# The first layer's scan as masked triangular products over blocks of 31 positions

## The chip, the core and the metric

The kernel runs on one core of one Trainium2 chip. TensorE (PE) multiplies matrices and transposes, with its weight loads (PEld) listed by themselves; VectorE (DVE) and ScalarE (ACT) work element by element and can read PSUM, into which TensorE writes; GpSimd (POOL) works on SBUF alone; SyncE (SP) issues the transfers (DMA). The metric is device time in microseconds of one launch, lower being better.

## What is computed

Two layers, each with a residual: group norm, a projection into a branch u and a gate, a state-space scan of u in four directions, a layer norm times the silu of the gate, and a projection back. The change is in the first layer's scan. Cut to that:

```python
# per batch (4), direction k (4), channel d (384), state n (16), along L = 4096 positions
xs = stack([x_hw, x_wh, flip(x_hw), flip(x_wh)])      # rows, columns, both reversed
x_dbl = einsum('bkdl,kcd->bkcl', xs, x_proj_weight)   # 12 rows for the step, 16 B, 16 C
delta = softplus(einsum(dts, dt_projs_weight) + bias)
As = -exp(A_logs)                                     # A_logs = log(1..16) for every channel
def step(h, inp):
    dA = exp(dt[..., None] * A_k[None])
    dBu = dt[..., None] * bt[:, :, None, :] * ut[..., None]
    h = dA * h + dBu
    y = einsum('bkdn,bkn->bkd', h, ct)
    return (h, y)
```

The outputs of the four directions are turned back to the order of the image and added, with u times the sum of the four D vectors. All data is f32.

## The kernel before

`FirstLayer.run` goes through the four batches one after another. `between` (L451) does what lies around the scans: `finish_steps` of the batch before, interleaved with `project_steps` (L529) of the batch to come. A projection normalizes the batch (`norm`), then handles 8 chunks of 512 positions: u by `in_proj` (L519), transposes of u (L545) into uT and into y times the D sum, and the rows of step, B and C for both orders (L556). The gate isn't projected there: `scans` does it on the side (`gate_in`, L791 writes it out).

`scans` takes 32 items (4 directions x 8 chunks of 512 positions) with 16 states each, so 512 steps a batch and 2048 in all. A step holds 3 x 128 channels by 512 positions:

- ACT multiplies the transposed dt*u by B (`b_product`, L716, four instructions) and takes exp(dt*A) (`decay`, L728, three);
- TensorE transposes the product, 12 blocks of 128 x 128, into PSUM (`turn_x`, L733);
- DVE runs the recurrence itself, one `tensor_tensor_scan` for each 128 channels (L741), and keeps the last column as a carry (L751);
- POOL multiplies h by C (L755), whose rows come from DRAM broadcast over the partitions;
- TensorE transposes h back, 12 blocks, adding over the 16 states in PSUM (`add_y`, L763).

The preparation of an item (`Item.steps`) is spread over the steps of the items before it: dt by small products (L632), softplus in parts on ACT and POOL (L638 to L658), dt*u (L681). The order on TensorE, ACT, DVE and POOL is written out by hand (`manual_schedule`); SP's is not. The second layer (`SecondLayer`, a subclass that uses `norm`, `in_proj`, `finish` and `finish_steps`) runs after all batches are done, and a flag `alive` decides at the end whether a general version of it is run too.

Of the kernel before, what the change touches and what calls it, by code (L numbers as in the profile page):

```python
# [19 lines left out]
LC = 512  # L20
# [8 lines left out]
ALL_ZERO = -105.0  # L29

# [372 lines left out]
class FirstLayer:  # L403

    def __init__(self, tc, ctx, consts, w, gate, dram):
        nc = tc.nc
        self.tc, self.w = tc, w
        self.ident, self.group, self.one = consts  # L410
        self.gate = gate
        self.uT_dram, self.ys, self.xp_dram = dram
        wp = ctx.enter_context(tc.tile_pool(name="wf", bufs=1))

        def load(name, shape):
            t = wp.tile(shape, F32, name=f"{name}_f")
            nc.sync.dma_start(t, w[name])
            return t

        self.w_xp = load("w_xq2", [128, ND, 2, 2 * NX])  # L420
        self.w_dt = load("w_dtb", [DR + 1, KD, DI])
        self.gamma = load("gamma", [128, ND])
        self.beta = load("beta", [128, ND])
        self.A = load("A_log", [128, KD, ND, NS])
        nc.scalar.activation(self.A, self.A, AF.Exp)
        nc.vector.tensor_scalar_mul(self.A, self.A, -1.0)
        self.xbias = load("x_bias2", [2 * NX, 1])
        self.ln_eps = wp.tile([128, 1], F32, name="ln_eps_f")
        nc.vector.memset(self.ln_eps, 1e-6)
        self.gn_eps = wp.tile([128, 1], F32, name="gn_eps_f")  # L430
        nc.vector.memset(self.gn_eps, GN_EPS)
        self.dsum = wp.tile([128, DI], F32, name="dsum_f")
        with tc.tile_pool(name="d4", bufs=1) as pd:
            d4 = pd.tile([128, KD, DI], F32, name="d4")
            nc.sync.dma_start(d4, w["D_rows"].partition_broadcast(128))
            nc.vector.tensor_add(self.dsum, d4[:, 0, :], d4[:, 1, :])
            nc.vector.tensor_add(self.dsum, self.dsum, d4[:, 2, :])
            nc.vector.tensor_add(self.dsum, self.dsum, d4[:, 3, :])

    def run(self, srcs, dsts):  # L440
        with self.tc.tile_pool(name="xT", bufs=1) as px:
            self.xT = px.tile([CB, NC2, L], F32, name="xT")
            self.w_in = px.tile([CB, NC2, 2 * DI], F32, name="w_in")
            self.bias = px.tile([128, 2 * ND], F32, name="bias")
            for b in range(len(srcs) + 1):
                self.between([(srcs[b - 1], dsts[b - 1], self.ys[b - 1], self.gate)] if b else [], srcs[b : b + 1], b)
                if b < len(srcs):
                    self.y_dram = self.ys[b]
                    self.scans()

    def between(self, done, todo, b):  # L451

        tc = self.tc
        with ExitStack() as ctx:
            pool = lambda name, bufs, **k: ctx.enter_context(tc.tile_pool(name=name, bufs=bufs, **k))
            psum = lambda name, bufs: pool(name, bufs, space=bass.MemoryType.PSUM)
            steps = []
            if done:
                sbuf = pool("fy", 8), pool("fz", 3), pool("fl", 2), pool("fs", 1), pool("fw", 2)
                banks = (2, 2) if todo else (4, 4)  # L460
                steps.append(self.finish_steps(done, sbuf, (psum("fm", banks[0]), psum("fo", banks[1])), pool("fc", 1)))
# [4 lines left out]
            while steps:  # L466
                for g in list(steps):
                    if next(g, None) is None:
                        steps.remove(g)
# [1148 lines left out]
```

## Time and profile before

| | |
|---|---|
| three runs | 11,063.09 us median, 11,059.26 to 11,072.16 |
| span of the profiled execution | 11,060.3 us |
| instructions | 169,780 |
| mean granted TensorE clock | 0.918 |
| HBM read, written | 955.83 MB, 300.42 MB |

How a page is read: busy time of an engine is the union of its instructions; the groups that follow give line, engine, operation, output and inputs, shape, count, then busy time, mean ns of one, and the idle time of the engine before them with what ended it. A mean can hold overlap with the neighbour, above all on TensorE, whose ends are modelled; there the spacing of neighbours in time is the cost. In the timeline, a line is one stretch: start, length, engine, line, operation, count. In a table of stretches each line gives the busy time and instructions of each engine, the granted clock and the DMA share.

The rows that the change touches, besides those shown below: L632 (the products for dt, 13 rows of weights, 512 columns) is 881.8 us busy in 1536 records; L641 and L652, an exponential and a logarithm of 128 x 1536 on ACT, take 1478 and 1485 ns; L645, a scalar operation of that size on POOL, 1480 ns; L681 and L778 on DVE, 128 x 512 with one input in PSUM, 674 ns; L549, 384 columns, 554 ns; L547, a copy of 384 columns out of PSUM on ACT, 483 ns.

### The profile page before, as it was taken

Reading aid. Unit: us, or ns where it says so; the run is one execution under the profiler, and the core shown is the slowest. Engines: PE = TensorE matmul, PEld = TensorE weight load, DVE = VectorE, ACT = ScalarE, POOL = GpSimd, SP = SyncE. Lnnn points to the kernel's source line nnn. Section 1 sums busy time; section 2 is a strip of 40 time slices with the busy share of each in tenths; the row PEclk is TensorE's granted clock in tenths of the full one; section 3 lists DMA queues with packets and bytes.
Section 4 is the critical chain, followed back from the end, with each engine's and each line's share of the span. In section 5 each row is a group of like instructions: output and inputs, shape, how many; then the busy total and the mean of one; then the engine's idle time right before and its main releaser. Section 6 shows DMA issues by size and latency. Waiting matters only on the chain. (4 is left out here: it accounts for less than half of the span.)

```text
span 11060.3 us, 169780 instructions
## 1 busy us (share of the span) xinstructions
PE 9381.9 (85%) x60297; PEld 7300.4 (66%) x60297; DVE 9708.2 (88%) x11512; ACT 9816.8 (89%) x17003; POOL 8590.8 (78%) x2776
## 2 busy tenths in 40 slices
PE   7888888888888888888888888888888888778677
PEld 4776776666777776656776766657767766644366
DVE  4999999976999999968999999959999999879675
ACT  5999999977999999968999999959999999867477
POOL 3999999955999999938999999929999999700370
PEclk8999999988999999998999999989999999988688
DMA  3333344444333444443433444443333444433458
GB/s 123 108 108 98 98 98 100 98 142 127 108 105 97 101 98 98 100 163 106 109 101 98 100 99 98 99 166 109 106 98 98 99 101 98 123 116 124 159 130 277
DMA packets 833662, 1267.39 MB, mean 115 GB/s; under 512 B 102026, under 2 KB 517655, under 8 KB 832292
## 3 DMA queue, kind: packets, MB, share of 16 engines
q1 hardware_dynamic: 827940, 1250.15, 41.6%
q0 software_dynamic: 4864, 6.29, 0.4%
q8 instruction: 479, 7.85, 0.3%
q14 instruction: 379, 3.10, 0.1%
HBM read 955.83 MB, written 300.42 MB: 114 GB/s over the span
## 5 line engine op out<-in xcount | busy, mean ns | idle before, releaser
L755 POOL TENSOR_TENSOR h<-h,bct 128x1536 f32<-128x1536 f32 x2048 | 7066.0, 3473 | 550.0 <-DVE carry L751 508.2
L741 DVE TENSOR_TENSOR_SCAN h<-a,carry,x 128x512 f32<-128x512 f32 x5376 | 6615.6, 1267 | 274.7 <-PE x L733 224.1
L733 PE MATMUL x<-ident,xT 128*128 128x128 f32 x24576 | 4118.0, 293 | 982.4 <-DVE h L741 881.1
L716 ACT ACTIVATE xT<-dtuT,bT 128x384 f32<-128x384 f32 x8192 | 4358.2, 609 | 34.7 <-PE x L733 29.7
L733 PEld LDWEIGHTS x<-ident,xT 128*128 128x128 f32 x24576 | 2888.9, 148 | 2170.3 <-DVE h L741 1013.3
L728 ACT ACTIVATE a<-dt,A_log_f 128x512 f32<-128x512 f32 x6144 | 3976.7, 716 | 0.0
L763 PE MATMUL yp<-ident,h 128*128 128x128 f32 x24576 | 3839.9, 285 | 9.2 <-POOL h L755 9.2
L763 PEld LDWEIGHTS yp<-ident,h 128*128 128x128 f32 x24576 | 3079.1, 149 | 11.1 <-POOL h L755 11.1
L632 PE MATMUL dp<-xd,w_dtb_f 13*128 13x512 f32 x1536 | 881.8, 657 | 201.5 <-DVE dt L661 198.4
L741 DVE TENSOR_TENSOR_SCAN h<-a,x 128x512 f32<-128x512 f32 x768 | 897.4, 1207 | 103.2 <-ACT a L728 70.6
L645 POOL TENSOR_SCALAR wl<-e 128x1536 f32<-128x1536 f32 x128 | 189.4, 1480 | 793.8 <-ACT e L641 600.3
L519 PE MATMUL pp<-xT,w_in 96*128 96x512 f32 x1152 | 542.1, 619 | 21.8 <-ACT pad L1109 21.0
L632 PEld LDWEIGHTS dp<-xd,w_dtb_f 13*128 13x128 f32 x1536 | 232.4, 187 | 441.7 <-DVE dt L661 327.7
L638 ACT ACTIVATE e<-dp 128x512 f32<-128x512 f32 x384 | 225.0, 586 | 288.9 <-DVE dt L661 191.1
L1123 DVE SCALAR_TENSOR_TENSOR acc<-pad,conv_w_s,acc 128x2048 f32<-128x2048 f32 x192 | 440.6, 2342 | 46.2 <-ACT acc L1121 44.9
L658 POOL TENSOR_TENSOR e<-e,wl 128x1536 f32<-128x1536 f32 x128 | 445.4, 3480 | 0.3
L1104 POOL MEMSET pad<- 128x66 f32 x12 | 1.9, 160 | 570.9 <-DVE acc L1123 446.0
L655 POOL TENSOR_TENSOR e<-e,dt 128x1536 f32<-128x1536 f32 x128 | 443.2, 3463 | 0.3
L519 PEld LDWEIGHTS pp<-xT,w_in 96*128 96x128 f32 x1152 | 221.4, 199 | 264.9 <-issue 232.0
L751 DVE TENSOR_REDUCE carry<-h 128x3 f32<-128x3 f32 x2048 | 322.8, 158 | 70.4
L661 DVE SCALAR_TENSOR_TENSOR dt<-dp,e 128x512 f32<-128x512 f32 x384 | 255.6, 666 | 64.8 <-POOL e L658 58.2
L931 PE MATMUL op<-w_out,v 128*128 128x192 f32 x1536 | 292.1, 340 | 10.1 <-DVE v L921 7.1
(168 smaller groups left out, 6366.1 us busy)
## 6 DMA issues: line engine op xcount, KB each, us to landing
bct<-xp SPq DMA_DIRECT2D x1024, 512.0 KB, 5.0
uT<-uT SPq DMA_DIRECT2D x64, 768.0 KB, 4.7
yold<-y SPq DMA_DIRECT2D x64, 768.0 KB, 7.9
y<-yt SPq DMA_DIRECT2D x64, 768.0 KB, 4.5
uT<-uT SPq DMA_DIRECT2D x128, 384.0 KB, 5.3
yold<-y SPq DMA_DIRECT2D x128, 384.0 KB, 6.9
y<-yt SPq DMA_DIRECT2D x128, 384.0 KB, 4.6
zg<-gate SPq DMA_DIRECT2D x64, 768.0 KB, 5.6
```

The source lines that it names most:

```text
L519: self.tc.nc.tensor.matmul(pp, self.w_in[:, i, e * 128 : (e + 1) * 128], self.xT[:, i, t * LC : (t + 1) * LC], start=(i == 0), stop=(i == ...
L632: nc.tensor.matmul(self.dp[d], w, self.xd[0 : DR + 1, :], start=True, stop=True)
L655: nc.gpsimd.tensor_tensor(self.e, self.e, self.dt, ALU.subtract)
L658: nc.gpsimd.tensor_tensor(self.e, self.e, self.wl, ALU.add)
L716: nc.scalar.mul(xTs[g][:, j, :], it.dtuT[:, j * DI : (j + 1) * DI], it.bT[:, j, n : n + 1])
L728: nc.scalar.activation(as_[g][:, d, :], it.dt[:, d, :], AF.Exp, scale=scale)
L733: nc.tensor.transpose(xs[g, d][:, j * 128 : (j + 1) * 128], xTs[g][:, j, d * 128 : (d + 1) * 128], ident)
L741: nc.vector.tensor_tensor_scan(along(hs[g][:, d, :], it.k), along(as_[g][:, d, :], it.k), along(xs.pop((g, d)), it.k), 0.0 if it.first els ...
L751: nc.vector.tensor_reduce(kept, last(hs[g], it.k), mybir.AxisListType.X, ALU.max)
L755: nc.gpsimd.tensor_tensor(hs[g], hs[g], bc(cs[g - n % 2][:, n % 2, :], 1, ND), ALU.mult)
L763: nc.tensor.matmul(it.yp[b][:, i * 128 : (i + 1) * 128], hs[g][:, d, j * 128 : (j + 1) * 128], ident, start=n == 0 and i == 0, stop=n == N ...
L1123: nc.vector.scalar_tensor_tensor(acc, part(tap), weight(tap), acc, ALU.mult, ALU.add)
```

## The change

`FirstLayer` no longer goes batch by batch. `run` projects all four batches, then scans all batches and directions together, then finishes all batches. What `FirstLayer` and `SecondLayer` share moves into a class `Stage`.

In the new `scans` the 128 partitions hold 4 directions x 31 positions (`NP` = 124) and four more rows, one for each direction, for the state carried from block to block; the 1536 columns are 4 batches x 384 channels. A round is one block of 31 positions in each direction (133 rounds), and each has 16 steps, one for each state, 2128 steps in all. With cum, the running sum of dt in the block (less a shift of 2.5), state n of the recurrence is exp(-n cum) times the running sum of B dt u exp(n cum). The factor exp(n cum) isn't computed for each state: `grown` multiplies what state n-1 had by g = exp(cum) once more. The running sum over positions, with B, is a product with a 128 x 128 triangular mask times B (`b_mask`, `mix`), one product for each batch; `weigh` multiplies the result by C and by exp(-n cum); `add_y` adds the states in PSUM by products with the identity. The carry rows go out to DRAM after each step and come back 16 steps later.

This needs A to be n times the same value, and the sum of dt over a block to stay small. `FirstLayer` checks both (and that the variance is finite) and keeps the outcome in `good`; if it fails, the general version of both layers is run at the end. There is thus a second branch behind the kernel.

```diff
+RW = 31
+NR = -(-L // RW)
+NP = KD * RW
+W = NB * DI
+SHIFT = 2.5
+REACH = 118.0
...
+    def run(self, srcs, dsts, gates):
+        self.project(srcs, gates)
+        self.scans()
+        self.reach()
+        self.finish([(src, dst, (self.y_row[:, b, :], self.y_col[:, b, :]), gates[b]) for b, (src, dst) in enumerate(zip(srcs, dsts))])
+
+    def load_y(self, y, t, py, pl, pos):
...
+        nc.sync.dma_start(yt, pos(y[0], t))
...
+        for s in range(2):
+            nc.sync.dma_start(yc[s * HW : (s + 1) * HW], v[s])
+        nc.gpsimd.tensor_tensor(yt, yt, yc, ALU.add)
...
+    def reach(self):
...
+            nc.sync.dma_start(t, self.tot.rearrange("(p f) -> p f", p=128))
...
+            nc.vector.tensor_reduce(top, t, mybir.AxisListType.X, ALU.max)
+            nc.vector.tensor_scalar(top, top, REACH / NS - SHIFT, None, ALU.is_le)
...
+    def project(self, srcs, gates):
...
+                    for e in range(ND):
+                        nc.scalar.activation(u[:, e, :], in_proj(e, t), AF.Identity, bias=bias[:, e : e + 1])
...
+                        for e in range(ND):
+                            nc.tensor.transpose(q[:, e * 128 : (e + 1) * 128], u[:, e, part], self.ident)
+                        nc.scalar.copy(ut[:, j, :], q)
+                        nc.vector.tensor_mul(du[:, j, :], q, self.dsum)
+                        for e in range(ND):
+                            nc.tensor.matmul(
+                                bp[:, j, :], u[:, e, part], self.w_bc[:, e, :], start=(e == 0), stop=(e == ND - 1)
+                            )
...
+                    for e in range(ND):
+                        nc.tensor.matmul(xp, self.w_xd[:, e, :], u[:, e, :], start=(e == 0), stop=(e == ND - 1))
...
+                    for e in range(ND):
+                        nc.scalar.activation(zg[:, e, :], in_proj(ND + e, t), AF.Identity, bias=bias[:, ND + e : ND + e + 1])
...
+            p_x, p_e, p_t, p_b = pool("bx", 7), pool("be", 4), pool("bt", 4), pool("bb", 3)
+            ps_y = pool("psy", 1, space=bass.MemoryType.PSUM)
+            ps_q = pool("psq", 3, space=bass.MemoryType.PSUM)
...
+                def v(self, i):
+                    self.vp = ps_m.tile([128, LC], F32, name="vp", tag="m")
+                    nc.tensor.matmul(self.vp[:NP, :DI], xd[:, i, :], w_dt, start=True, stop=True)
...
+                    nc.scalar.activation(self.e[:, cols(i)], self.vp[:NP, :DI], AF.Abs)
+                    nc.scalar.activation(self.dt[:, cols(i)], self.vp[:NP, :DI], AF.Relu)
...
+                    terms = ((ident, self.e), (minus, self.d), (ident, self.l), (ident, self.dt))
+                    for j, (m, t) in enumerate(terms):
+                        nc.tensor.matmul(self.dp[:NP, :DI], m[:NP, :NP], t[:, cols(i)], start=j == 0, stop=j == 3)
...
+                    nc.tensor.matmul(self.cp[:, :DI], tri[:NP], self.dt[:, cols(i)], start=True, stop=True)
...
+                    r = [(-31, "sp", self.load_xd), (-22, "sp", self.load_u), (-11, "sp", self.load_bc)]
+                    r += [(-15, "act", self.exp), (-14, "act", self.log), (-14, "pool", self.plus)]
+                    for i in range(NB):
+                        r += [(i - 20, "pe", s(self.v, i)), (i - 19, "act", s(self.parts, i))]
+                        r += [(i - 13, "pe", s(self.delta, i)), (i - 12, "dve", s(self.times_u, i))]
+                        r += [(i - 12, "act", s(self.keep_dt, i)), (i - 8, "pe", s(self.sums, i))]
+                        r += [(i - 7, "act", s(self.keep_sums, i))]
+                    r += [(-3, "act", self.grow), (-2, "first", self.grow_psum), (-2, "sp", self.keep_total)]
+                    r += [(6, "sp", self.load_y), (NS + LAG + 1, "sp", self.store_y)]
+                    for j in range(ND):
+                        r += [(NS + LAG, f"dve{j}", s(self.end_y, j))]
...
+            def decay(s):
+                it, n = of(s)
+                es[s] = p_e.tile([128, W], F32, name="e")
+                nc.scalar.activation(es[s], it.cum, AF.Exp, scale=-(n + 1.0))
+
+            def b_mask(s, i):
...
+                if i < 2:
+                    nc.scalar.mul(bs[s][:, i, :], mask, b)
+                else:
+                    nc.gpsimd.tensor_scalar(bs[s][:, i, :], mask, b, None, ALU.mult)
+
+            def grown(s, engine):
+                it, n = of(s)
+                part = slice(0, FREE) if engine is nc.vector else slice(FREE, W)
+                x = it.dtu if n == 0 else xs[s - 1][:NP]
+                g = it.g0[:NP, :FREE] if engine is nc.vector else it.g
+                engine.tensor_tensor(xs[s][:NP, part], x[:, part], g, ALU.mult)
+
+            def mix(s, i):
+                qs[s, i] = ps_q.tile([128, LC], F32, name="q")
+                nc.tensor.matmul(qs[s, i][:, :DI], bs[s][:, i, :], xs[s][:, cols(i)], start=True, stop=True)
+
+            def weigh(s, i):
...
+                nc.vector.scalar_tensor_tensor(
+                    ts[s][:, cols(i)],
+                    qs.pop((s, i))[:, :DI],
+                    it.bc[:, i, NS + n : NS + n + 1],
+                    es[s][:, cols(i)],
+                    ALU.mult,
+                    ALU.mult,
+                )
+
+            def add_y(s, j):
...
+                nc.tensor.matmul(
+                    it.yp[j],
+                    ident,
+                    ts[s][:, j * LC : (j + 1) * LC],
+                    start=n == 0,
+                    stop=n == NS - 1,
+                    skip_group_check=True,
+                )
...
+                for s in range(-LEAD, N + LAG + 3):
+                    on = lambda q: 0 <= q < N
+                    if on(s - 1):
+                        carry_out(s - 1)
+                    if on(s + 4):
+                        carry_in(s + 4)
+                    planned(s, "sp")
+                    planned(s, "first")
+                    if on(s + 2):
+                        decay(s + 2)
+                        b_mask(s + 2, 0)
+                        b_mask(s + 2, 1)
+                    planned(s, "act")
+                    if on(s + 2):
+                        grown(s + 2, nc.gpsimd)
+                        b_mask(s + 2, 2)
+                        b_mask(s + 2, 3)
+                    planned(s, "pool")
+                    for i in range(NB):
+                        if on(s):
+                            weigh(s, i)
+                        planned(s, f"dve{i}")
+                        if i == 1 and on(s + 2):
+                            grown(s + 2, nc.vector)
+                    planned(s, "dve")
+                    for i in range(NB):
+                        if on(s + 1):
+                            mix(s + 1, i)
+                        if i > 0 and on(s - LAG):
+                            add_y(s - LAG, i - 1)
+                    planned(s, "pe")
```

SP's order is now written by hand as well. The gate is projected in `project`, with the rest, into one DRAM array for each batch; the finish loads two sums, by rows and by columns, where it loaded one.

## The prediction

> **What bounds the kernel now.** I began with the busy table at the head of the page, then took one of the four scan stages by itself, then the costliest groups, and last the order in time on TensorE. The head of the page and the scan stages of the first two batches (columns: from and to, length, then busy time and instructions of PE, weight loads, DVE, ACT and POOL, granted clock, DMA share, GB/s):
>
> ```profile
> PE 9381.9 (85%) x60297; PEld 7300.4 (66%) x60297; DVE 9708.2 (88%) x11512; ACT 9816.8 (89%) x17003; POOL 8590.8 (78%) x2776
> ...
> 205.00:2370.00 2165.00, 1885.57 (x13095) 1527.34 (x13095) 2063.01 (x2330) 2100.43 (x3713) 2033.18 (x628) 0.95 0.40 100
> 2610.00:4790.00 2180.00, 1900.02 (x13175) 1537.95 (x13176) 2078.26 (x2347) 2113.95 (x3737) 2051.17 (x632) 0.94 0.39 100
> ```
>
> In a scan stage ACT is 97% busy, DVE 95%, POOL 94%, PE 87%. A batch has 512 steps, and 2180/512 is 4.26 us a step. No single engine sets it; all four are loaded to nearly the same level, so a change must be added up for every engine. These groups make up the step:
>
> ```profile
> L755 POOL TENSOR_TENSOR h<-h,bct 128x1536 f32<-128x1536 f32 x2048 | 7066.0, 3473 | 550.0 <-DVE carry L751 508.2
> L741 DVE TENSOR_TENSOR_SCAN h<-a,carry,x 128x512 f32<-128x512 f32 x5376 | 6615.6, 1267 | 274.7 <-PE x L733 224.1
> L733 PE MATMUL x<-ident,xT 128*128 128x128 f32 x24576 | 4118.0, 293 | 982.4 <-DVE h L741 881.1
> L716 ACT ACTIVATE xT<-dtuT,bT 128x384 f32<-128x384 f32 x8192 | 4358.2, 609 | 34.7 <-PE x L733 29.7
> L728 ACT ACTIVATE a<-dt,A_log_f 128x512 f32<-128x512 f32 x6144 | 3976.7, 716 | 0.0
> L763 PE MATMUL yp<-ident,h 128*128 128x128 f32 x24576 | 3839.9, 285 | 9.2 <-POOL h L755 9.2
> ```
>
> All of TensorE's work in a step is transposes: 12 at L733 and 12 at L763 (24576/2048), one record each. What one costs is read from its neighbours in time, since the mean of 293 ns overlaps with the next. In the scan, weight loads of four come 0.44 us apart (columns: start, length, engine, line):
>
> ```profile
> 1201.52 0.47 PEld L733 LDWEIGHTS x<-ident,xT 128*128 128x128 f32 x4
> ...
> 1201.96 0.47 PEld L763 LDWEIGHTS yp<-ident,h 128*128 128x128 f32 x4
> ...
> 1202.40 0.47 PEld L733 LDWEIGHTS x<-ident,xT 128*128 128x128 f32 x4
> ```
>
> So a 128-column transpose takes 110 ns, and the step 24 x 0.11 = 2.64 us of TensorE. Ordinary f32 products are another matter, and the change is made of them. The projections show them. Two things are to be seen: how many records one product leaves, and how far apart they are.
>
> ```profile
> L556 PE MATMUL xp<-u,w_xq_f 128*128 128x512 f32 x384 | 178.0, 593 | 0.0
> ```
>
> L556 runs 3 products for 2 orders, 8 chunks and 4 batches: 192 products, yet 384 records. An ordinary f32 product is two records, each with its own weight load; a transpose is one. L519's gate products (192, 384 records) and L931's (768, 1536 records) say the same. The spacing of a dense row of 512-column records, and of 192-column ones:
>
> ```profile
> 10002.13 0.19 PEld L519 LDWEIGHTS pp<-xT,w_in 96*128 96x128 f32 x1 [0.24 <-issue]
> 10002.56 0.19 PEld L519 LDWEIGHTS pp<-xT,w_in 96*128 96x128 f32 x1 [0.24 <-issue]
> 10002.99 0.19 PEld L519 LDWEIGHTS pp<-xT,w_in 96*128 96x128 f32 x1 [0.24 <-issue]
> ...
> 10999.70 10.48 PE L931 MATMUL op<-w_out,v 128*128 128x192 f32 x55
> ```
>
> 512 columns: 430 ns a record, the 190 ns load hidden behind the product before. 192 columns: 10.48/55 = 190 ns a record, the length of the load. So a 512-column product costs 0.86 us. The granted clock of such dense stretches:
>
> ```profile
> 80.00:90.00 10.00, 9.99 (x33) 5.09 (x32) 3.87 (x6) 3.10 (x6) 0.00 (x0) 1.00 0.50 185
> 90.00:100.00 10.00, 9.99 (x33) 4.97 (x32) 3.80 (x6) 3.10 (x6) 0.00 (x0) 1.00 0.50 184
> ```
>
> **The change, part by part.** The four scan stages (181.5 us, the first scan, to about 2380; the last ends at 9636; some 2195 us each), the three stages between them (some 222 us each) and the first projection go. In their place stand one projection of all batches, 133 rounds x 16 = 2128 steps, and one finish.
>
> *TensorE in a step.* mix is four products of 384 columns, add_y three of 512. A 384-column record is in no row of before: in proportion to 512 it is 322.5 ns; on the line through 190 (192 columns) and 430 it is 334. I take 322.5, since 190 is the load's length and not the product's; the other end adds (8 + 3) x 11.5 ns x 2128 = 270 us. mix: 8 x 322.5 = 2.58 us. add_y: 6 x 430 = 2.58 us. Each round adds v 4, delta 16, sums 4, 24 products of 384 columns or 48 records: 15.48 us, 0.97 a step. Together 6.13 us a step against 2.64 before; 133 rounds of 98.0 us are 13,039 us.
>
> *The other engines in a step* lie behind that. POOL: the 1152-column product, 2605 ns by proportion to L755 or 2718 on the line through 1461 ns for 512 columns (L1302); two masks of 128 columns, each between 160 ns (a memset of 66) and 1480 ns (L645, 1536), taken near the small end as 300; plus, 1480/16. Sum 3.3 us, and with every upper end 5.8. ACT: decay 1478 (L641), two masks between 303 (L1131, 128 columns) and 609 (L716), a sixteenth of the round's 8 x 483 + 1478 + 1485 + 4 x 483 + 4 x 580 + 1108 + 500 (483 from L547, 580 from L540's 686 by 384 of 512 columns and its start, 1485 from L652): 2.9 to 3.5 us. DVE: five of 384 columns at 554 (L549) and a sixteenth of 4 x 554 + 3 x 674: 3.0 us. SP issues some 70 transfers a round (32 carries, 4 xd, about 9 each for u and bc, about 6 and 8 for y, 1 total); before, they follow each other on its queue at 0.32 to 0.45 us, so 32 of 98 us. If TensorE did not cover them, POOL would be next at 3.3 us.
>
> *Waits added.* mix waits for the masks and for grown, one step older on ACT and POOL, and for one of three q buffers, which weigh frees. DVE needs 3 us in 6. end_y for a round sits between the weighs and holds the three y banks, which the next round's first add_y needs; 0.67 us each, and TensorE has two mixes (1.3 us) in front of it. The carry is read back 12 steps after it was written, 70 us; queued behind a late one on SP would be u, bc and y, for which whole steps are free. I price these at 1% of the stage, 130 us: between none (9.99 of 10 us above) and the 5% that PE missed in a dense stretch of the second layer (47.71 of 50 us at 9950).
>
> *Projection.* To the first product, 40 us as now. A chunk has 15 products of 512 columns (in_proj 6 for u and 6 for the gate, now out in the open, xp 3): 30 x 0.43 = 12.9 us; 12 transposes, 1.4; 12 products of 128 columns for B and C, 24 records at the load's 190 ns, 4.6. 18.9 x 32 = 604. Three more norms at some 15: 45. Sum 689. ACT (6 us) and DVE (5 us a chunk) are hidden.
>
> *Around the scan.* Filling took about 60 us before (135 to 195); I keep it, and 10 for draining. reach loads 3.3 MB, which at the finish's 316 GB/s is 10 us, and a reduction: 15.
>
> *Finish.* The second layer's finish moves 2.36 MB a chunk and takes 239 us for 32 chunks (10821 to the end), at a DMA share near 0.95: transfers set it. The column sums add 0.79 MB a chunk: 239 x 3.15/2.36 = 319 us. POOL's added sum, 3.5 us a chunk, is hidden.
>
> *The rest.* Second layer from about 9722 to the end: 1338, and 5 for the second flag. The sum of any 31 neighbouring step sizes, worked out from the reference's inputs, is at most 4.9, below the 7.4 that the flag allows, so the general path isn't run.
>
> Sum: 689 + 60 + 13,039 + 10 + 130 + 15 + 319 + 1343 = 15,605 us of the profiled execution, whose own span of before, 11,060.3, is 3 us under the median of the runs; so 15,600.
>
> Two statements of the Trainium skill bear on this. "TensorE: Matmul & The Clock Gate", section "Back-to-back issue gap", gives a sustained 131 ns for 512 columns; by it a step would need, as an estimate, some 2.2 us of TensorE, POOL would set it at 3.3, and the whole would be near 9,700. The rows say 430 ns twice, and they decide. The same page, "Part 1: The HAM clock gate", has a limiter that takes the clock to 13/16 once three cores of a die run dense products; one core runs here, so by it nothing is added, and no run here shows a dense stretch of 13 ms.
>
> **The rivals.**
> *A lower clock.* The scan stages of before ran at 0.95, not 1.00, but with gaps of 13% in PE. If the new one stays at 0.95: 13,039/0.95, 690 more: 16,300. For it: no stretch of before shows 13 ms at 1.00. Against: every dense 10 us does.
> *TensorE isn't fed.* If weight loads come out into the open because each product waits on its own signal: 8.5 products x 190 ns = 1.6 us more a step, 18,900 to 19,000. For it: before, loads of L733 idled 2170 us. Against: those waited for h, 1013 us; in L519 and L931 the loads run ahead.
> *Faster.* If the products with the square mask or the identity as weights leave one record like the transposes, TensorE needs 3.06 us, POOL sets the step at 3.3 to 3.6: 2128 x 3.45 + 2436, about 9,800. It decides as soon as a pair of records costs less than 66% of what it does at L519: with 2,436 us in the other stages, a step may last 4.05 us for the end to stay under 11,063. Against: L556 and L931 have full f32 operands of 128 rows, and are doubled.
> *The general path runs.* Its scan has 32 x 8 groups a batch, each with two 3072-column products (3.5 us by L921's 1747 ns for 1536) and six scans of 1.27 us on DVE, 14.6 us: 15 ms, and as much for the second layer, which the flag sends there too, so over 40 ms in all; the bound of 4.9 against 7.4 excludes it but for an error of mine.
>
> **How the numbers follow.** TensorE sets it, clock 1.00: 0.75 (own range 15,300 to 16,000). Lower clock: 0.12. Not fed, or another queue: 0.08. Faster: 0.03. General path: 0.01. No change: 0.01; 0.2% is about what a measurement of this kernel can tell from none. The lower end: no gaps and a fill half as long, with 50 us off projection and finish, 15,400; 15,250 leaves room. The upper: 334 ns a record and the 0.95 clock, 15,605 + 270 + 690, about 16,600.
>
> **What would show it.** mix with 17,024 records at a spacing near 322 ns, add_y with 12,768 at 430; PE over 97% busy through a stage of some 13.1 ms at a clock of 1.00; DVE, ACT and POOL near half; rounds of 98 us. I am wrong if mix leaves 8,512 records, if PE idles on weigh, grown or a DMA, or if the clock in the stage is under 0.97.

## The result, and the profile after

The changed kernel takes 15,719.9 us (median; 15,715.9 to 15,736.3) beside 11,066.5 us of the kernel before: a ratio of 1.421, with a 95% interval of 1.419 to 1.423. The forecast was 15,600. The profiled execution has a span of 15,734.5 us. The head of its page:

```profile
PE 15096.9 (96%) x44314; PEld 7960.0 (51%) x44314; DVE 7993.0 (51%) x13687; ACT 7158.9 (45%) x11063; POOL 9177.8 (58%) x6769
```

TensorE's instructions fell from 60,297 to 44,314, and its busy time rose from 9,382 to 15,097 us. Before, four engines stood between 78 and 89%; now three stand at about half and one at 96%. The stages of the changed kernel, from its windows (from and to, length, busy time and instructions of PE, weight loads, DVE, ACT, POOL, granted clock, DMA share, GB/s): the scan, the finish of the first layer, and the second layer:

```profile
728.00:13950.00 13222.00, 13222.00 (x36122) 6750.28 (x36122) 6608.78 (x11564) 5804.45 (x9017) 8753.14 (x6517) 1.00 0.14 31
13950.00:14376.00 426.00, 204.65 (x1154) 182.50 (x1152) 193.79 (x471) 209.87 (x280) 110.55 (x32) 0.71 0.94 240
14376.00:15734.00 1358.00, 1013.99 (x4506) 667.33 (x4506) 986.82 (x1296) 896.62 (x1348) 302.55 (x212) 0.82 0.51 159
```

In the scan TensorE has no idle time at all, 13,222 of 13,222 us, at a clock of 1.00. That is one stage that one engine sets. The finish is another kind: every engine is idle for half of it or more, and the DMA share is 0.94. The groups of the step:

```profile
L959 PE MATMUL q<-x,b 128*128 128x384 f32 x17024 | 6591.5, 489 | 0.0
L978 PE MATMUL yp<-t,ident 128*128 128x512 f32 x12768 | 6518.0, 592 | 0.0
L955 POOL TENSOR_TENSOR x<-x,g 124x1152 f32<-124x1152 f32 x1995 | 5269.2, 2641 | 0.0
L948 POOL TENSOR_SCALAR b<-mask_f,bc 128x128 f32<-128x128 f32 x4256 | 2538.7, 612 | 3933.7 <-PE q L959 3933.7
L827 POOL TENSOR_SCALAR d<-e 124x1536 f32<-124x1536 f32 x133 | 718.0, 5399 | 688.2 <-ACT e L823 688.2
```

mix left 17,024 records, 8 a step, and add_y 12,768, 6 a step: two for each product. The idle time on TensorE ahead of both is 0.0, and what idles is POOL, for mix. A mean of 489 or 592 ns overlaps with the next record; what a product costs is read from the starts in time. One plain step on TensorE, from its first mix to the next step's:

```profile
5015.05 1.45 PE L959 MATMUL q<-x,b 128*128 128x384 f32 x4
5016.34 1.02 PE L978 MATMUL yp<-t,ident 128*128 128x512 f32 x2
5017.20 0.81 PE L959 MATMUL q<-x,b 128*128 128x384 f32 x2
5017.85 1.02 PE L978 MATMUL yp<-t,ident 128*128 128x512 f32 x2
5018.70 0.81 PE L959 MATMUL q<-x,b 128*128 128x384 f32 x2
5019.35 1.02 PE L978 MATMUL yp<-t,ident 128*128 128x512 f32 x2
5020.21 1.45 PE L959 MATMUL q<-x,b 128*128 128x384 f32 x4
```

Four mix records last 5016.34 - 5015.05 = 1.29 us, 322.5 ns each; two of add_y 0.86, 430 ns each; the step 5.16 us.

### The profile page after: what moved, and what is told of

Same layout as the page of the kernel before. It is cut to its first block, busy times and chain, and to the rows that moved or that the text cites. A ratio compares the mean times of both kernels' runs of the same rounds, so it can differ in the third digit from the quotient of the medians.

```text
span 15734.5 us, 156576 instructions
## 1 busy us (share of the span) xinstructions
PE 15096.9 (96%) x44314; PEld 7960.0 (51%) x44314; DVE 7993.0 (51%) x13687; ACT 7158.9 (45%) x11063; POOL 9177.8 (58%) x6769
## 5 line engine op out<-in xcount | busy, mean ns | idle before, releaser
L965 DVE SCALAR_TENSOR_TENSOR t<-q,bc,e 128x384 f32<-128x384 f32 x8512 | 5151.6, 616 | 4688.1 <-PE q L959 3893.9
L959 PE MATMUL q<-x,b 128*128 128x384 f32 x17024 | 6591.5, 489 | 0.0
L978 PE MATMUL yp<-t,ident 128*128 128x512 f32 x12768 | 6518.0, 592 | 0.0
L955 POOL TENSOR_TENSOR x<-x,g 124x1152 f32<-124x1152 f32 x1995 | 5269.2, 2641 | 0.0
L959 PEld LDWEIGHTS q<-x,b 128*128 128x128 f32 x17024 | 3183.8, 190 | 3440.9 <-issue 2589.6
L948 POOL TENSOR_SCALAR b<-mask_f,bc 128x128 f32<-128x128 f32 x4256 | 2538.7, 612 | 3933.7 <-PE q L959 3933.7
L978 PEld LDWEIGHTS yp<-t,ident 128*128 128x128 f32 x12768 | 2425.3, 190 | 1694.6 <-issue 4.3
L938 ACT ACTIVATE e<-cum 128x1536 f32<-128x1536 f32 x2128 | 3152.0, 1481 | 197.4 <-DVE t L965 197.4
L946 ACT ACTIVATE b<-mask_f,bc 128x128 f32<-128x128 f32 x4256 | 1457.7, 392 | 396.9 <-PE q L959 396.9
L827 POOL TENSOR_SCALAR d<-e 124x1536 f32<-124x1536 f32 x133 | 718.0, 5399 | 688.2 <-ACT e L823 688.2
L955 DVE TENSOR_TENSOR x<-x,g 124x384 f32<-124x384 f32 x1995 | 1083.8, 543 | 0.0
```

Of the source, the lines that this page charges most:

```text
L827: nc.gpsimd.tensor_scalar(self.d, self.e, 1.0, -1.0, ALU.add, ALU.add)
L938: nc.scalar.activation(es[s], it.cum, AF.Exp, scale=-(n + 1.0))
L946: nc.scalar.mul(bs[s][:, i, :], mask, b)
L948: nc.gpsimd.tensor_scalar(bs[s][:, i, :], mask, b, None, ALU.mult)
L955: engine.tensor_tensor(xs[s][:NP, part], x[:, part], g, ALU.mult)
L959: nc.tensor.matmul(qs[s, i][:, :DI], bs[s][:, i, :], xs[s][:, cols(i)], start=True, stop=True)
```

## The experiments

Times are of the whole kernel, in us; the changed kernel's is 15,720, and its four runs lie some 20 us apart. e1, e8, e9, e10 and e11 are medians of four runs, the others single runs. e2, e3, e4 and e7 change what comes out: e2 leaves states out, e3 takes the wrong B, e4 and e7 mix up the order of y.

| run | edit to the changed kernel | theory | measured |
|---|---|---|---|
| e1_v128 | v's 52 rows filled up to 128 | 15,515 | 15,508 |
| e2_half_adds | half of add_y left out | 12,975 | 13,180 |
| e3_masks_twice | POOL's masks left out | 15,720 | 15,698 |
| e4_turned_adds | add_y as transposes | 13,040 | 13,112 |
| e7_yc_rows | column sums read in contiguous order | 15,630 | 15,623 |
| e12_plus_two | plus as two instructions | 15,720 | 15,708 |
| e5_adds_r | add_y in float32r | 12,975, or 11,700 to 12,000 | 11,860 |
| e8_light_r | and lighter preparation | 10,070, or 11,430 | 11,524 |
| e9_psum_r | and DVE's operands in PSUM | 9,970 to 10,720 | 10,586 |
| e10_two_r | and the sum on TensorE | 10,720 | 10,888 |
| e11_later_r | e9 with one addition later | 10,170 to 10,310 | 10,327 |

**Is TensorE the bound, and alone?** Two runs take work from it, one takes work from POOL.

```diff
# e2_half_adds, in add_y
+                if n % 2:
+                    return
...
-                    stop=n == NS - 1,
+                    stop=n == NS - 2,
# e3_masks_twice
-                        b_mask(s + 2, 2)
-                        b_mask(s + 2, 3)
...
-                nc.tensor.matmul(qs[s, i][:, :DI], bs[s][:, i, :], xs[s][:, cols(i)], start=True, stop=True)
+                nc.tensor.matmul(qs[s, i][:, :DI], bs[s][:, i % 2, :], xs[s][:, cols(i)], start=True, stop=True)
# e4_turned_adds, in add_y
-                nc.tensor.matmul(it.yp[j], ident, ts[s][:, j * LC : (j + 1) * LC], ...)
+                for i in range(NJ):
+                    at = j * LC + i * 128
+                    nc.tensor.matmul(it.yp[j][:, i * 128 : (i + 1) * 128], ts[s][:, at : at + 128], ident,
+                                     start=n == 0 and i == 0, stop=n == NS - 1, is_transpose=True, ...)
```

> add_y is left out for every second state, so half of the states are missing from y; all other engines do the same work. Theory (TensorE alone sets the scan): 133 x 8 times 6 records x 430 ns = 2.58 us go, 2,745 us in all; a round falls from 99.55 to 78.9 us and the time to 12,975, with PE still at 97 to 100% and POOL at 66 x 99.55/78.9 = 83%. Rival 1 (the step hangs on the chain grown, mix, weigh or on POOL's 4.2 us as much as on TensorE): the mean step can't fall below 5.5 us or so, the gain is under 1,500 us, 14,200 or more, with gaps in PE. Rival 2 (weigh gives up q so late that TensorE's add_y was filling a wait): no change, 15,720.

> POOL's two masks a step are left out, and the products of batches 2 and 3 take the masks of batches 0 and 1, so their B is a wrong one. POOL loses 2 x 612 ns of some 4.2 us a step. Theory (TensorE is the bound and POOL is covered): no change, 15,720 within 40, PE at 100% in the scan, POOL at 46% in place of 66%. Rival (POOL's bursts, plus at 5.4 us above all, hold back grown or the masks in some steps): the time falls by up to 133 x 1.2 = 160 us or more, 15,560 or less.

> add_y's three products of 512 columns become twelve transposes of 128 columns that add up in the same banks; y so comes out turned in its blocks of 128 by 128 and isn't turned back. Theory (a transpose is one record of 110 ns, also when it adds into a bank, where a product of 512 columns is two of 430): add_y costs 12 x 0.11 = 1.32 us in place of 2.58, 1.26 x 2128 = 2,680 us go, the time is 13,040 and a plain step 3.90 us. Rival 1 (each record of 128 columns is held to the 190 ns of its weight load, since these weights change every time): 12 x 0.19 = 2.28 us, 640 us go, 15,080. Rival 2 (a transpose that adds is doubled as well): 12 x 0.38 = 4.56 us, 4,210 us more, 19,930.

The scan's window of e2, with TensorE's wait ahead of mix from the groups under it:

```profile
728.00:11407.00 10679.00, 10580.28 (x29724) 5479.37 (x29722) 6392.67 (x11559) 5769.67 (x9007) 8732.80 (x6511) 1.00 0.17 38
```

```profile
L959 PE MATMUL q<-x,b 128*128 128x384 f32 x17024 | 6305.2, 492 | 98.7 <-DVE t L965 98.7
```

2,540 of the 2,745 us went. TensorE is busy for 10,580 of 10,679 us: with a fifth less work it begins to wait for weigh, 99 us that count as idle. The rest shows in the starts of the records: from one mix record to the next, what goes beyond 323 ns adds up over the scan to 255 us in e2 and to 65 in the changed kernel. That is 190 of the 205 us that are missing; a wait that is shorter than the modelled end of a record counts as busy. So close to a fifth of TensorE's time can go before the next wait shows. e3 shows the reverse: POOL's busy time in the scan falls by 2,470 us and nothing happens.

```profile
728.00:13920.00 13192.00, 13192.00 (x36050) 6735.58 (x36049) 6595.01 (x11538) 5792.72 (x9000) 6283.29 (x2259) 1.00 0.14 30
```

In e4 the order on TensorE is the same, and each add_y is now four transposes:

```profile
5007.41 0.60 PE L980 MATMUL yp<-ident,t 128*128 128x128 f32 x4
5007.84 0.81 PE L959 MATMUL q<-x,b 128*128 128x384 f32 x2
5008.49 0.60 PE L980 MATMUL yp<-ident,t 128*128 128x128 f32 x4
```

Four take 0.43 us from their start to the next, 110 ns each, also where they add into a bank, against 0.86 us for the same 512 columns as a product. The kernel before had this already: its add_y at L763 is made of such transposes, which add over the 16 states, and the prediction read 0.44 us for four. Of the time, 2,608 us went for 2,681 expected. That an f32 product costs two records is what the change pays for.

**The exposed weight load.** The v product is the one that didn't fit: a step with v lasts 6.19 us. TensorE's products and weight loads around it in the changed kernel (start, length; in brackets the time since the load before ended):

```profile
5001.82 1.02 PE L978 MATMUL yp<-t,ident 128*128 128x512 f32 x2
5002.77 0.91 PE L813 MATMUL vp<-w_dtk_f,xd 52*124 52x384 f32 x2
5003.60 1.56 PE L959 MATMUL q<-x,b 128*128 128x384 f32 x4
5005.00 1.02 PE L978 MATMUL yp<-t,ident 128*128 128x512 f32 x2
```

```profile
5002.77 0.29 PEld L813 LDWEIGHTS vp<-w_dtk_f,xd 52*124 52x124 f32 x2 [0.76 <-issue]
5003.60 0.94 PEld L959 LDWEIGHTS q<-x,b 128*128 128x128 f32 x4 [0.55 <-issue]
```

Neither v's own load, nor the load of mix behind it, runs ahead under the product before, as the others do. From start to start the records of add_y ahead of v take 0.95 us in place of 0.86, v 0.83 in place of 0.645, and the four of mix behind it 1.40 in place of 1.29: 0.385 us more in all. v is the only product here with 52 rows.

```diff
-            xd = p1.tile([KD * DR + KD, NB, NP], F32, name="xd")
-            nc.sync.dma_start(xd, self.w["grid"])
+            xd = p1.tile([128, NB, NP], F32, name="xd")
+            nc.vector.memset(xd, 0.0)
+            nc.sync.dma_start(xd[: KD * DR + KD], self.w["grid"])
+            w_dt = p1.tile([128, DI], F32, name="w_dt128")
+            nc.vector.memset(w_dt, 0.0)
+            nc.vector.tensor_copy(w_dt[: KD * DR + KD], self.w_dt)
```

> v's operands are filled up from 52 to 128 rows with zeros; nothing else is changed and the values are the same. In the changed kernel a step with v lasts 6.19 us and a plain step 5.16 us, so v takes 1.03 us where the other products of 384 columns take 0.645. Theory (TensorE is the bound, and a product whose rows differ from its neighbours' loads its weights in the open): v falls to 0.645, 0.385 x 4 x 133 = 205 us go, a round goes from 99.55 to 98.0 us, and the time to 15,515. Rival 1 (v waits for xd, or for the one PSUM bank that it shares with delta and sums): the 1.03 us stay, 15,720. Rival 2 (only the load ahead of v is in the open, and the one behind it is due to the change of bank): about half, 15,620.

The ratio to the kernel before falls from 1.421 to 1.401 (1.399 to 1.403), by 212 us. TensorE in e1, around v:

```profile
5013.79 1.02 PE L982 MATMUL yp<-t,ident 128*128 128x512 f32 x2
5014.65 0.81 PE L817 MATMUL vp<-w_dt,xd 128*124 128x384 f32 x2
5015.29 1.45 PE L963 MATMUL q<-x,b 128*128 128x384 f32 x4
```

v is back at 5015.29 - 5014.65 = 0.64 us: more than twice the rows, and less time. But not every change in the number of rows costs something, as the theory has it. The products of delta and sums have 124 rows and stand between products of 128, and in the changed kernel they cost no more than the others, 5067.28 - 5066.63 = 0.65 us:

```profile
5066.63 0.81 PE L849 MATMUL cp<-dt,tri_f 124*128 124x384 f32 x2
5067.28 1.45 PE L959 MATMUL q<-x,b 128*128 128x384 f32 x4
```

What sets 52 rows apart from 124 was not tried.

**The finish.** Why 426 us for a stretch forecast at 334?

```diff
-        n = LC // HW
-        v = y[1].rearrange("(w h) e -> h w e", h=HW)[t * n : (t + 1) * n].rearrange("(j s) w e -> s w j e", s=2)
-        for s in range(2):
-            nc.sync.dma_start(yc[s * HW : (s + 1) * HW], v[s])
+        nc.sync.dma_start(yc, pos(y[1], t))
```

> The finish reads the column sums in the order in which it reads the row sums (both then in pieces of 1,536 bytes that lie 6,144 bytes apart, where the column sums' neighbouring pieces lie 64 x 6,144 = 393,216 bytes apart now), as one transfer in place of two; so rows and columns of the image are mixed up in y. The same bytes are moved. In the changed kernel the stretch from the last add_y to the second layer took 426 us, at 249 GB/s and 117 ns a packet of 1,536 bytes, where the forecast had 334. Theory (the wide stride is what slows the packets): the stretch falls to about 334 us, the time to 15,630. Rival (pieces of 1,536 bytes out of the four batches' rows are slow at any distance, or the added traffic itself): the stretch stays within 20 us of 426, the time at 15,720.

POOL's sum of the two in the finish, of the changed kernel and then of e7 (busy, mean; idle time before it and what ended it):

```profile
L652 POOL TENSOR_TENSOR yt<-yt,yc 128x1536 f32<-128x1536 f32 x32 | 110.5, 3456 | 277.9 <-DMA yc<-y_col 218.9 <-DMA yt<-y_row 54.7 <-ACT yt L525 4.2
```

```profile
L649 POOL TENSOR_TENSOR yt<-yt,yc 128x1536 f32<-128x1536 f32 x32 | 115.6, 3620 | 184.0 <-DMA yc<-y_col 87.5 <-DMA yt<-y_row 52.7 <-ACT yt L525 42.2
```

The stretch falls to 326 us. The same bytes go at 309 GB/s in place of 240, and a packet of 1,536 bytes takes 70 ns in place of 116 (mean over such packets of the trace in this stretch). So the way of reading costs the 100 us: neighbouring pieces 393 KB apart against 6 KB, and two transfers of 64 partitions against one. The run changed both, and which of the two it is stays open.

**POOL's plus.** It took 5,399 ns where the forecast had 1,480.

```diff
-                    nc.gpsimd.tensor_scalar(self.d, self.e, 1.0, -1.0, ALU.add, ALU.add)
+                    nc.gpsimd.tensor_scalar(self.d, self.e, 1.0, 1.0, ALU.add, ALU.mult)
+                    nc.gpsimd.tensor_scalar(self.d, self.d, -1.0, 1.0, ALU.add, ALU.mult)
```

> POOL's plus, d = (e + 1) - 1 in one instruction with two additions, becomes two instructions of an addition and a multiplication by 1 each, as the kernel before has them (1,480 ns each for 128 x 1536); the values are the same. In the changed kernel the one instruction takes 5,399 ns. Theory (the pair of operations sets its time): 2 x 1,480 = 2,960 ns a round on POOL in place of 5,399, and no change of the time, 15,720 within 40, since TensorE covers POOL. Rival 1 (the length is due to what runs beside it, or to the 124 partitions): two instructions of 5,400 ns each, 10.8 us a round, and still 15,720, or more if POOL then comes late. Rival 2 (a first addition on POOL takes 2,700 ns whatever follows): 5,400 in all.

```profile
L828 POOL TENSOR_SCALAR d<-d 124x1536 f32<-124x1536 f32 x133 | 195.8, 1472 | 11.6
L827 POOL TENSOR_SCALAR d<-e 124x1536 f32<-124x1536 f32 x133 | 195.5, 1470 | 685.3 <-ACT e L823 685.3
```

Two instructions are together 2.5 us shorter than the one. The pair of operations sets the time; TensorE covers it either way.

**A version that beats both.** If two records a product are the price, a type with one record should lower it.

```diff
+            ident_r = p1.tile([128, 128], mybir.dt.float32r, name="ident_r")
+            nc.vector.tensor_copy(ident_r, ident)
...
-                    ts[s] = p_t.tile([128, W], F32, name="t")
+                    ts[s] = p_t.tile([128, W], mybir.dt.float32r, name="t")
...
-                    ident,
+                    ident_r,
```

> weigh writes its products as float32r, a float32 rounded for TensorE, and add_y multiplies them by an identity of that type; y's addends and the carried rows are so rounded, nothing else is changed. Theory (TensorE is the bound, and the 2.58 us of add_y come from each product being two records): with one record of 430 ns add_y costs 1.29 us, 2,745 us go, 12,975; with one record of 215 ns (a transpose takes 110 ns for 128 columns, so about 0.43 us for 512 at its rate; 215 is half of an f32 record) it costs 0.65 us, TensorE would need 4.25 us a step and POOL 4.2, so 11,700 to 12,000 with gaps in PE. Rival 1 (the type changes nothing: two records of 430 ns): 15,720. Rival 2 (weigh takes longer when it rounds, or the step hangs on its chain): over 13,300 with PE under 97% in the scan.

```profile
5004.95 0.81 PE L961 MATMUL q<-x,b 128*128 128x384 f32 x2
5005.30 0.69 PE L980 MATMUL yp<-t,ident_r 128*128 128x512 f32 x1
5005.83 0.81 PE L851 MATMUL cp<-dt,tri_f 124*128 124x384 f32 x2
```

One record, and from one mix to the product behind add_y 5005.83 - 5004.95 = 0.88 us, of which mix is 0.645: 0.23 us for 512 columns in place of 0.86. The time is 11,860, in the scan TensorE is busy for 99% and POOL for 93%: the next engine is right behind. So the next step lightens POOL and TensorE together.

```diff
# e8_light_r, on top of e5_adds_r and e1_v128
-                def plus(self): ...
                 def delta(self, i):
-                    for j, (m, t) in enumerate(terms):
-                        nc.tensor.matmul(self.dp[:NP, :DI], m[:NP, :NP], t[:, cols(i)], ...)
+                    nc.vector.tensor_add(self.dt[:, cols(i)], self.dt[:, cols(i)], self.l[:, cols(i)])
...
-                    nc.vector.tensor_mul(self.dtu[:, cols(i)], self.dp[:NP, :DI], ut[:, cols(i)])
+                    nc.vector.tensor_mul(self.dtu[:, cols(i)], self.dt[:, cols(i)], ut[:, cols(i)])
...
-                if i < 2:
+                if i < 3:
                     nc.scalar.mul(bs[s][:, i, :], mask, b)
```

> A version meant to beat both. On top of add_y in float32r: v's operands filled up to 128 rows; the step size is ln(1 + e) + relu on DVE (one addition of 384 columns a batch), so plus on POOL, delta's 16 products a round and keep_dt on ACT go, and with them the correction of the rounding of 1 + e; the third mask moves from POOL to ACT. Estimates of a step from the rows of the changed kernel: TensorE 2.58 + 0.65 + 8 x 0.645/16 = 3.55 us (4.19 if a float32r record takes 430 ns), POOL 2.64 + 0.61 = 3.25, ACT 1.48 + 3 x 0.39 + 0.55 = 3.2, DVE 4 x 0.616 + 0.54 + 0.4 = 3.4. Theory (TensorE sets the step as long as the others stay below it): 2128 x 3.55 + 728 + 426 + 1358 = 10,070, or 11,430 at 430 ns a record; some per cent more for waits, since four engines are then nearly level. Rival 1 (with four engines level the waits between them set the step, as they did in the kernel before, 4.26 us): 11,580, no gain over the kernel before. Rival 2 (POOL's product of 1152 columns, which goes through its own slow path, still hides behind nothing): a step of 3.9 us or more, 10,800.

11,524 us, a ratio of 1.042 (1.040 to 1.043): my theory's time is missed by 1,450 us, and the first rival's 11,580 nearly met. But it is not the level of the four engines that sets it. TensorE stood 1,011 us ahead of mix for weigh, so DVE was late, the engine that I had at 3.4 us a step:

```profile
L955 PE MATMUL q<-x,b 128*128 128x384 f32 x17024 | 6805.9, 502 | 1015.1 <-DVE t L961 1010.9 <-POOL x L951 3.2
```

The cause is in two operations that here have both operands in SBUF: the addition of the step size's terms, which TensorE made in the changed kernel, and the product with u, which read one operand from PSUM there. POOL and DVE of e8, side by side:

```profile
5011.49 0.60 POOL L944 TENSOR_SCALAR b<-mask_f,bc 128x128 f32<-128x128 f32 x1
5012.06 2.70 POOL L951 TENSOR_TENSOR x<-x,g 124x1152 f32<-124x1152 f32 x1
5016.91 0.60 POOL L944 TENSOR_SCALAR b<-mask_f,bc 128x128 f32<-128x128 f32 x1 [2.15 <-PE q L955]
5017.48 2.64 POOL L951 TENSOR_TENSOR x<-x,g 124x1152 f32<-124x1152 f32 x1
```

```profile
5011.71 0.56 DVE L841 TENSOR_TENSOR dtu<-dt,ut 124x384 f32<-124x384 f32 x1
5012.19 2.99 DVE L836 TENSOR_TENSOR dt<-dt,l 124x384 f32<-124x384 f32 x1
...
5016.16 0.54 DVE L951 TENSOR_TENSOR x<-x,g 124x384 f32<-124x384 f32 x1
...
5017.67 2.86 DVE L841 TENSOR_TENSOR dtu<-dt,ut 124x384 f32<-124x384 f32 x1
```

The operation at 5011.71 began beside one of POOL's short masks and took 0.56 us. The next began 0.13 us behind POOL's product and ended at 5015.18, 0.42 us after POOL's end at 5014.76; the one at 5017.67 likewise, 0.41 after 5020.12. DVE did most of its own work after POOL's, and weigh stood behind it. The whole trace says the same: of the 210 additions that began while POOL's product ran, 209 ended 0.41 to 0.43 us after it, and of 285 such products with u 276 did; the other 322 additions took 0.67 us at most. The Trainium skill, "SBUF — State Buffer", section "Who interferes with whom", says it in advance: a DVE instruction with two inputs in SBUF contends with a GpSimd instruction that reads SBUF, and the later of the two is blocked until the other has ended. These rows agree for POOL's product. For its masks, which read SBUF too, the measurement says otherwise: 383 of the two operations began beside one, and none took over 0.7 us.

The changed kernel avoids it: every operation of its step on DVE has an operand in PSUM, grown's factor for DVE's share (grow_psum) among them. e9 and e10 give DVE such operands again, in two ways, and store the column sums in the order of the rows, a way of reading that took 100 us off the finish in e7:

```diff
# e9_psum_r
+                    nc.scalar.activation(self.lp[:NP, :DI], self.e[:, cols(i)], AF.Ln, bias=one[:NP])
...
+                    nc.vector.tensor_add(part, self.lp[:NP, :DI], part)
...
+                    nc.gpsimd.tensor_tensor(self.dtu[:, cols(i)], self.dt[:, cols(i)], ut[:, cols(i)], ALU.mult)
# e10_two_r: delta as in the changed kernel, with
+                    terms = ((ident, self.l), (ident, self.dt))
# both, in load_y and store_y
-                        for row, lo, n in runs(k, r):
-... (y_row, y_col)[k % 2][lo : lo + n]
+                        for row, lo, n in runs(k, r, k % 2 == 1):
+... place((y_row, y_col)[k % 2], k, lo, n)
```

> The version before (add_y in float32r, lighter preparation) again, but so that DVE never takes two operands from SBUF: ACT writes ln(1 + e) into PSUM a batch at a time, DVE adds it there to relu, and the product with u goes to POOL; the correction of the rounding of 1 + e is left out as before. The column sums are also stored in the order of the rows, so that the finish reads pieces 6,144 bytes apart. In the version before, DVE's two operations of 384 columns on operands in SBUF took 1,511 and 1,740 ns, from 543 (alone) to 3,852, where the same with one operand in PSUM takes 544, and they ended with POOL's product; mix then waited 1,011 us for weigh. Theory (DVE with two SBUF operands waits for POOL's whole instruction): both go to 0.55 us or to POOL (0.9 us each), a step is 3.55 to 3.9 us, and with 334 us in the finish the time is 2128 x 3.55 to 3.9 + 728 + 334 + 1358 = 9,970 to 10,720. Rival (four engines at 3.3 to 3.55 us a step hold each other up whatever the operands): a step as in the version before, 4.2 us, 11,400.

> As the last, but the step size's two terms, ln(1 + e) and relu, are added by TensorE as in the changed kernel (two products of 384 columns in place of four), and DVE and ACT read the sum from PSUM as there. TensorE: 2.58 + 0.65 + 16 x 0.645/16 = 3.87 us a step; POOL 3.25, ACT 3.3, DVE 3.2. Theory (DVE's wait for POOL is gone and TensorE sets the step again): PE over 96% busy in the scan, 2128 x 3.9 + 728 + 334 + 1358 = 10,720. Rival (the waits are not due to the operands): 4.2 us a step, 11,400.

10,586 us, 0.957 (0.955 to 0.959) of the kernel before, and 10,888, 0.984 (0.983 to 0.986). DVE's addition is at 554 ns, and TensorE at 96 and 99% in the scan. e10 is 170 us over its forecast. What e9 still lost was seen on DVE:

```profile
5032.48 0.69 DVE L879 TENSOR_TENSOR yt<-yp,yold 124x512 f32<-124x512 f32 x1 [0.26 <-PE yp L974]
5034.93 0.56 DVE L836 TENSOR_TENSOR dt<-lp,dt 124x384 f32<-124x384 f32 x1 [1.75 <-ACT lp L832]
5035.40 0.61 DVE L961 SCALAR_TENSOR_TENSOR t<-q,bc,e 128x384 fp32r<-128x384 f32 x1
```

The addition stands 1.75 us for ACT, and weigh, which TensorE needs, is behind it in DVE's queue. TensorE in the same step, the next product after its wait, for which the profile names no releaser:

```profile
5036.11 1.16 PE L955 MATMUL q<-x,b 128*128 128x384 f32 x2 [1.91 <-issue]
```

```diff
-... (i - 14, "dve0", s(self.delta, i)), (i - 12, "pool", s(self.times_u, i))]
+... (i - 13, "dve0", s(self.delta, i)), (i - 11, "pool", s(self.times_u, i))]
```

> As e9_psum_r, but DVE's addition of a batch's step size comes one step later, and POOL's product with u too; the same operations and values. In e9_psum_r a plain step takes 3.27 us on TensorE, and in the step of the first addition DVE stood 1.75 us for ACT's ln(1 + e), behind it weigh, and TensorE stood 1.91 us and more for q and x: PE 96% busy, some 2.7 us of 70 a round missing. Theory (DVE's queue stands behind that one wait): most of it goes, 133 x 2 to 3 us = 270 to 400 us, 10,170 to 10,310, PE at 98 to 99% in the scan. Rival (POOL, at 89%, is what TensorE waits for): within 100 us of 10,585.

The scan of e9, then that of e11:

```profile
720.00:8886.00 8166.00, 7844.04 (x25485) 4849.65 (x25484) 6436.93 (x11548) 6269.81 (x10987) 7296.63 (x4777) 0.98 0.23 49
720.00:8638.00 7918.00, 7763.05 (x25484) 4781.10 (x25483) 6388.32 (x11547) 6249.90 (x10993) 7312.06 (x4779) 1.00 0.23 51
```

10,327 us, 0.934 (0.932 to 0.935) of the kernel before: 258 us less than e9, just short of what was expected. The scan is 7,918 us with TensorE at 98%, POOL at 92%. It is the fastest here, at the price of float32r for the addends of y and of leaving out the correction of the rounding of 1 + e. What the two take of y's accuracy was not measured.

The wait in e9 cost more than its own length. TensorE stands for 1.9 us once in each of e9's 133 rounds. In 88 of them the granted clock then falls to a half, mostly for 3.4 us and within 1 us of the end of the wait. The 185 records of TensorE that follow the wait in a round take 57.3 us (median) with such a stretch and 56.6 without. By that the clock has some 60 us of the 258 (an estimate, 88 x 0.7), which no forecast here had in its sum. In e11 two waits over 0.6 us are left once the scan runs, and with them two such stretches. e8's scan has 529 us at half clock; what that adds to its time was not separated.

## Why the prediction was right

The end was 15,735 us for a sum of 15,605 in the profiled execution. Stage by stage, in us:

| term | forecast | measured |
|---|---|---|
| up to the first mix (projection 689, filling 60) | 749 | 728 |
| the scan (13,039, gaps 130, draining 10) | 13,179 | 13,222 |
| reach and finish (15 + 319) | 334 | 426 |
| second layer (1338 + 5) | 1,343 | 1,358 |

- *TensorE's records.* Right in number and size: 17,024 and 12,768, at 322.5 and 430 ns. This carries the forecast; e4 and e5 show it from the other side. Of the two values for 384 columns the proportional one held, but not for the reason given. The row of 192 columns, read as 190 ns and as the load's length, is a mean over two clocks: its records are 320 ns apart at its beginning (a granted clock of 0.56 from 10,999 to 11,003 us) and 163 behind it, at 1.00. That is in proportion to 512 columns (161 ns) and shorter than the load. A record isn't held to 190 ns.
- *The waits at 130 us.* Wrong in kind. No wait for weigh, grown or a transfer showed in the scan. What filled the place is the step "24 products of 384 columns ... 15.48 us": v costs 1.03 us and not 0.645, 205 us by the steps, 212 by e1. The forecast had the exposed loads as a rival for all products at 1.6 us a step; they came for v's four of a round alone. They lie inside what the profile counts as busy; only the starts of the records show them. That the scan came within 43 us of its forecast is luck: 130 us for waits that didn't come stood where 205 us were missing.
- *The clock.* 1.00 through 13.2 ms of dense products, so the rival at 16,300 is out. It agrees with what the forecast took from the Trainium skill, "TensorE: Matmul & The Clock Gate", section "Part 1: The HAM clock gate": one core alone doesn't set off that limiter. The trace of before, with 0.95 in its scans, had left the rival open, and it wasn't without a ground: in e9 the clock did fall behind TensorE's waits.
- *The finish at 319 us.* The term was mis-sized: bytes by a rate from transfers whose pieces lie close, for pieces 393 KB apart, read in two transfers. 100 us, shown by e7 for both together.
- *The other engines.* DVE 6,609/2128 = 3.1 us a step and ACT 2.7, near the forecast. POOL's 3.3 us was wrong: 8,753/2128 = 4.1, from masks of 612 ns for an estimated 300 and a plus of 5,399 for 1,480. TensorE covers it. But the rival on the other side was priced with it: had all products been single records, POOL would have held the scan at 8,753 or so, and with 2,512 us of the other stages the time would be, as an estimate, 11,265, not 9,800, and still over the kernel before. The point from which it was to decide, two thirds of a pair, was so not enough alone. The 9,700 for 131 ns a product doesn't follow from the 3.3 us beside it either (2128 x 3.3 + 2436 = 9,458); the sum makes no use of it.
- *The start and the second layer.* -21 and +15 us. The first product came at 58 us, not 40. The projection then ran to 667 us, 609 for a forecast 649: the 768 records of 128 columns for B and C, priced at the load's 190 ns, came 111 ns apart as a rule and took 89 us in all for 146. Filling took 61 for 60. The 15 us of the second layer were not followed.

## What to carry to other kernels

Before a scan is turned into products, read from the trace how many records a product of that type leaves and how far apart they are: here the count of TensorE's instructions fell by a quarter and the time rose by 42%, and the type of one operand pair was worth 3,860 us. A margin under a covering engine should be costed as closely as the bound, since it decides what every later improvement is worth. When engines are nearly level, look first at what stands at the head of an engine's queue: DVE operations with both operands in SBUF cost TensorE 1,011 us of waiting, and one addition a step too early cost 258 us. And read the clock in the stretch behind a wait, not only in the mean: some 60 of those 258 us lay there, by the estimate from e9.

## What the runs showed of the hardware that was not expected

- A product with 52 rows between products of 128 costs 0.385 us more than the others, and its load and the next one don't run ahead. Filled up with zeros to 128 rows it takes 0.64 us, as the others do; with 124 rows products take 0.65.
- After a wait of 1.9 us TensorE's clock fell to a half, mostly for 3.4 us, in 88 of e9's 133 rounds.
- DVE operations with both operands in SBUF ended 0.41 to 0.43 us after the product of POOL beside which they began, in 485 of 495 cases of e8, but weren't held up by POOL's masks.
- A float32r product of 512 columns is one record of 0.23 us, where the f32 one is two and takes 0.86.
- POOL's instruction with two additions takes 5,399 ns for 124 x 1536; two with an addition and a multiplication take 1,470 each.
- POOL's product of a 128 x 128 tile with one value a partition takes 612 ns.
